# Gated attention block on one core: last group of the batch attention normalised by halves, logits ahead of the turned outputs, the values' bias taken through the head, PE's order at the router written by hand

## The chip, the core and the metric

The kernel runs on one core of a Trainium2 chip. The metric is the time of one execution in microseconds (us) of device time; the runs of the kernel before gave 2961.96, 2963.43 and 2974.54 us, so the median is 2963.43 us. One more execution was taken with the hardware profiler: it took 2965.17 us and its profiled span is 2963.4 us. Engines are called PE (matrix products and transposes), PEld (PE's weight loads), DVE (vector engine), ACT (scalar engine), POOL (GpSimd) and SP (the engine that issues the transfers); SPq is SP's queue.

## What is computed

The reference is one block of a gated cross-attention network over x of shape (8, 512, 256), all in float32, cut here to what the change touches:

```
x  = x + tanh(g_xattn[0]) * relational_cross_attention(layernorm(x), ctx, boxes)   # 16 heads
n  = layernorm(x)
y1 = ln(n + mha(n))                      # 4 heads, attends over the 8 batch rows' axis
gates = softmax(y1 @ wg); idx = argmax   # 8 experts, 512 tokens each
y2 = ln(y1 + gate * expert(y1))          # two matrix products per expert
x  = x + tanh(g_ffn[0]) * y2
q = layernorm(x) @ WQ.T + bQ;  k = ctx @ WK.T + bK;  v = ctx @ WV.T + bV
Z = softmax(q k.T / 16) @ v
x  = x + tanh(g_xattn[1]) * (tile(Z, 8) @ Wl.T + bl)
x  = x + tanh(g_ffn[1]) * spiking_ffn(layernorm(x))
```

Each row of softmax(q k.T / 16) sums to one, so the constant bV passes through it unchanged: Z = softmax(..) @ (ctx @ WV.T) + bV.

## The kernel before, in words

The work goes through four stages, one after the other. First the gated cross-attention with its projections (`project_all`, `gated_cross_attention`), up to about 1980 us of the span. Then `batch_attention`, about 1980 to 2215 us: 32 tiles of 128 tokens in NG = 8 groups of 4. Then `experts`, about 2215 to 2515 us, which begins with the router (`route`). Last comes `tail` (second cross-attention and spiking feed-forward).

**Batch attention.** The work of tile k = 4g + j is put out by `slot(k)`; PE, ACT, DVE and POOL follow the order of the code here (`manual_schedule`), SP's order is a planner's. A slot turns tile k-1's exponentials on PE (`turn`, L763), forms tile k's scores (L737), mixes tile k-2 (`mix`, L806 on PE, the residual sum `res` L807 on DVE), weighs tile k-1 with its values (`weigh`, L774 on PE, then `o` L780 on DVE) and turns these outputs on PE (`turn_out`, L793, copied by ACT L795 to `oT`). On DVE the scores are masked (`sm`, L742) and their maximum taken (`nm`, L748) before ACT exponentiates them (`e`, L752). Beside that, each of the four slots of a group carries a share of other groups: slot j = 0 turns the inputs of group g+1 (L689) and forms the logits of group g-3 (`logits`: 16 PE matmul records into `pl`, L845, and a DVE copy into `lg`, L849), slots 1 and 2 form queries and keys (L699), slot 3 the values (L715, bias added by DVE at L719). The output layer norm of group g-1 runs in slots 1 to 3: `out_stats` (L59 to L62: four pairs of statistics, one small sum, one power on POOL into `ln_rs`) and `out_norm` (two DVE instructions for each tile, L820 and L823, into `y`, and a write to DRAM, L824). `logits_turn` turns two tiles of y on PE (L832) and ACT copies them to `yT` (L836).

After each group, `late.sums(g)` and `late.load(g)` prepare weights of later stages: for g = 2 to 5 a DVE sum over a staged quarter of Wl (`wl`, L1166), for g = 2 also five scalings (L1151); the loads that `late.load` issues go through SP.

**The end of batch attention** (L913 on) finishes tiles 30 and 31, and puts between them the first pieces of other work: the keys and values of the last attention for batch 0, in four pieces by the generator `late.keys(0, ..)`. A piece of `key` is 4 PE matmul records (L1202), an ACT copy with bias into `kT` (L1207) and a write to `ckd`; a piece of `value` is 8 records (L1217), a DVE instruction that adds the bias into `v` (L1222) and a write to `cvd`. The last group's four tiles are normalised together after `out_stats(7)`, and the last `logits` closes the stage.

**Router and experts.** `route` is a chain of some fifty small DVE instructions: softmax and argmax over 8 experts (L986 to L1006, the exponential on ACT, L989), three matmuls that count tokens ahead of each token (`pc`, `pa`, `pb`, L1011 to L1017), a running sum (L1026, L1027), the place of each token (`loc`, `rest`, `col`), and 32 pairs of one-hot tiles (`rows` L1059, `cols` L1064 and L1068, in four parts) whose products on PE (L1072, `pt`) give the token list (`token`, L1076). POOL gathers the rows of each expert's tokens by it (L1261). The keys and values of batches 1 to 4 (`keys(..)`, before the loop over experts) are put out after the router's code, and the planner chooses where PE does them; only SP follows the code. Then 8 experts follow, each with transposes of its tokens (L1278, copied by DVE L1281), L1295 and L1304 on PE; and after them the values, then the keys, of batches 5 to 7 (L1319).

**Tail.** `fetch` gathers the experts' rows for 4 tiles on POOL (L1395); `combine` adds them on DVE (`z`, L1412), takes statistics (L1357 to L1360), adds (L1423, L1426), takes statistics again, and `ln_apply` (`xn`, L1367) gives what PE turns first (`features`, L1379). `head` multiplies by the summed Wl and adds `bl` (L1437).

Of the kernel before, what the change touches and what calls it, by code (L numbers as in the profile page):

```python
# [11 lines left out]
F32 = mybir.dt.float32  # L12
I32 = mybir.dt.int32
AF = mybir.ActivationFunctionType
ALU = mybir.AluOpType
# [4 lines left out]
P = 128  # L20
B, S, D = 8, 512, 256
# [596 lines left out]
def batch_attention(cx, a, y1, lg, x1q, y1d, xf0, late):  # L618
# [6 lines left out]
    with ExitStack() as es:  # L625
# [183 lines left out]

        def out_stats(g):  # L810
            if g >= 0:
                lns["r", g] = cx.stats(wk, ress[g], 4)

        def out_norm(g, j0, j1):
            if g < 0:
                return
            mv, rs = lns["r", g]
            for j in range(j0, j1):
                y = y1[:, 4 * g + j, :]
                nc.vector.scalar_tensor_tensor(  # L820
                    y, ress[g][:, j, :], mv[:, j, 0:1], g1, ALU.subtract, ALU.mult
                )
                nc.vector.scalar_tensor_tensor(y, y, rs[:, j : j + 1], b1, ALU.mult, ALU.add)  # L823
                nc.sync.dma_start(out=yg_[4 * g + j], in_=y)  # L824
# [32 lines left out]
        def slot(k):  # L857
# [6 lines left out]
            if j == 0:  # L864
                in_stats(g + 2)
                first, second = in_turn(g + 1, 0), in_turn(g + 1, 1)
                turn_out(k - 1)
                do(first)
                logits(g - 3)
            elif j == 1:  # L870
# [32 lines left out]
        with tc.manual_schedule(engines=MANUAL | {mybir.EngineType.Pool}):  # L903
# [9 lines left out]
            for g in range(NG):  # L913
                load(g + 3)
                for j in range(4):
                    slot(4 * g + j)
                late.sums(g)
                late.load(g)
            g = NG - 1
            fill = late.keys(0, staged)  # L920
            turn(NK - 1)
# [3 lines left out]
            logits_turn(g - 1, 0)  # L925
            turn_out(NK - 1)
            next(fill)
            logits_turn(g - 1, 2)
            mix(NK - 1)
            out_stats(g)  # L930
            logits(g - 1)
            next(fill)
            next(fill)
            out_norm(g, 0, 2)
            logits_turn(g, 0)
            next(fill)
            out_norm(g, 2, 4)
            logits_turn(g, 2)
            logits(g)


def route(cx, lg, order, pool, gkd):

# [8 lines left out]
    with ExitStack() as es:  # L952
# [151 lines left out]
class Late:  # L1104
# [66 lines left out]
    def load(self, g):  # L1171

        tc, nc, a, pool = self.cx.tc, self.cx.nc, self.a, self.pool
        if g == 1:

            self.matrix("order", "order", 3, P)
            self.matrix("wk", "WKT", 2, D)
            self.matrix("wv", "WVT", 2, D)
            self.matrix("wq", "WQT", 2, D)
            for name, key in (("bk", "bK"), ("bq", "bQ")):  # L1180
                self.w[name] = pool.tile([P, 2], F32, name=name)
                nc.sync.dma_start(out=self.w[name], in_=a[key])
            for name, key in (("bv", "bV"), ("bl", "bl"), ("g2", "g2"), ("b2", "b2ln")):
                self.vector(name, key)
            self.w["wl"] = pool.tile([P, 2, D], F32, name="wl")
# [24 lines left out]
    def value(self, b, m, tile):  # L1210

        nc, w = self.cx.nc, self.w
        pv = tile("p", [P, 2, D])
# [7 lines left out]
        v = tile("v", [P, 2, D])  # L1221
        nc.vector.tensor_tensor(v, pv, w["bv"].unsqueeze(1).to_broadcast([P, 2, D]), ALU.add)  # L1222
        nc.sync.dma_start(out=self.d["cv"][b][:, 2 * m : 2 * m + 2, :], in_=v)

    def keys(self, b, tile):
# [9 lines left out]
def experts(cx, lg, late, moe, gkd, y1d, yd, between):  # L1235

    tc, nc, ident = cx.tc, cx.nc, cx.ident
    with ExitStack() as es:
# [6 lines left out]

        def keys(*bs):
            for b in bs:
                for _ in late.keys(b, staged):
                    pass
# [16 lines left out]
        tokens(0)  # L1266
        keys(*range(1, late.LAST))
        for e in range(NE):
# [396 lines left out]
def flamingo_gated_block(ctx: ExitStack, tc: tile.TileContext, a, out):  # L1665
    nc = tc.nc
# [53 lines left out]
    with ExitStack() as es:  # L1720
# [11 lines left out]
        def load_x1(q):  # L1732
            if q < NQ:
# [59 lines left out]
def _layout(v):  # L1793
# [45 lines left out]
        "WVT": _rows(x["L1_xattn_WV"].T, 2),  # L1839
        "bV": x["L1_xattn_bV"],  # L1840
        "WlT": x["L1_xattn_Wl"].T.reshape(8, 2, P, D).transpose(2, 0, 1, 3),
# [22 lines left out]
```

## Time and profile before

| what | value |
|---|---|
| runs | 2961.96, 2963.43, 2974.54 us (median 2963.43) |
| profiled execution: its time | 2965.17 us |
| profiled execution: its span | 2963.4 us, mean granted clock of PE 0.989 |
| instructions | 39430 |
| PE busy | 2895.3 us (98%) |
| DVE busy | 1836.2 us (62%) |
| ACT busy | 1403.0 us (47%) |
| chain that ended last | PE 77%, DVE 15%, DMA 2% |
| hardware queue of transfers | 375.28 MB, 43.8% of 16 engines' span |

How to read it: a busy share is an average over stages with different limits, so what a change in one stage is worth has to be read from that stage. In a timeline row the first two columns are the start and the length in us, then the engine, the line of the code, the operation, `out<-in`, the sizes and the count; in brackets stands how long the engine had been idle before and what ended the wait. A row with a count above one merges neighbours and spans them all. In a row of stretches the columns are the stretch, its length, busy us and count for PE, PEld, DVE, ACT and POOL, then the clock that PE was granted (1.00 is full), the busy share of the transfer engines and the GB/s that they moved.

### The profile page before, as it was taken

To read this page: it belongs to the slowest core of one execution; us is meant where nothing else is said; L and a number is where in the kernel's file an instruction comes from. 1 tells how busy PE (TensorE), PEld (TensorE's weight loads), DVE (VectorE), ACT (ScalarE), POOL (GpSimd) and SP (SyncE) were. 2 spreads that over 40 slices of the span, in tenths; PEclk is the share of its full clock that TensorE was granted. 3 is DMA by queue.
4 is the path that set the end of the run, shared out by engine and by line. 5 is a ranking of instruction groups with operands and counts; after the bars stand their busy time and mean duration, and the time that the engine had idled before them with its cause. 6 is when DMAs were issued, how large, how long until landed. Compare 5 with 4: busy or idle time off the path is not lost.

```text
span 2963.4 us, 39430 instructions
## 1 busy us (share of the span) xinstructions
PE 2895.3 (98%) x15304; PEld 2118.9 (72%) x15304; DVE 1836.2 (62%) x2875; ACT 1403.0 (47%) x2196; POOL 138.2 (5%) x137
## 2 busy tenths in 40 slices
PE   8999999999999999999999999999989999899998
PEld 3444478888888888888888888867766666456566
DVE  6332177868777777777777777557753012666758
ACT  4332356665656565665656666335531211343434
POOL 2000000000000000000000000000002111212100
PEclk9999999999999999999999999999989999999999
DMA  7785546454545555555555555461113432211000
GB/s 228 222 235 168 184 117 166 132 166 133 163 137 156 143 153 143 155 141 153 146 151 149 144 153 140 127 199 50 43 58 127 156 124 85 100 45 56 30 15 22
DMA packets 269338, 386.18 MB, mean 130 GB/s; under 512 B 55176, under 2 KB 133000, under 8 KB 266336
## 3 DMA queue, kind: packets, MB, share of 16 engines
q1 hardware_dynamic: 266080, 375.28, 43.8%
q0 software_dynamic: 3072, 8.39, 1.0%
q8 instruction: 121, 1.98, 0.3%
q14 instruction: 65, 0.53, 0.1%
HBM read 237.36 MB, written 78.07 MB: 106 GB/s over the span
## 4 chain that ended last, share of the span: by engine, by line
PE 77%; DVE 15%; DMA 2%; issue 2%; ACT 1%; SPq 1%; POOL 0%; DVEq 0%; ACTq 0%; POOLq 0%
PE pg L448 12%; PE po L504 11%; PE pS L468 7%; PE pk L225 6%; PE pT L484 5%; PE ph L1512 4%; PE pw L535 4%; PE ph L1295 4%; PE py L1304 4%; PE py L1527 4%; PE pv L240 3%; DVE nm L472 2%; PE pz L1484 2%; DVE lt L345 2%; PE pq L699 2%
## 5 line engine op out<-in xcount | busy, mean ns | idle before, releaser
L475 ACT ACTIVATE e<-pS,nm 128x512 f32<-128x512 f32 x512 | 323.8, 684 | 577.3 <-DVE nm L472 576.7
L448 PE MATMUL pg<-wst,emb 116*128 116x208 f32 (+1 forms) x2560 | 582.3, 350 | 8.1 <-DVE gate L454 5.9
L448 PEld LDWEIGHTS pg<-wst,emb 116*128 116x128 f32 x2560 | 414.6, 190 | 205.6 <-issue 79.8
L504 PEld LDWEIGHTS po<-v,at 128*128 128x128 f32 x4096 | 493.0, 192 | 0.1
L504 PE MATMUL po<-v,at 128*128 128x65 f32 x4096 | 485.7, 272 | 0.0
L472 DVE TENSOR_REDUCE nm<-pS 128x2 f32<-128x1024 f32 x256 | 312.8, 1222 | 176.0 <-PE pS L468 176.0
L486 DVE SCALAR_TENSOR_TENSOR at<-gate,pT 128x1024 f32<-128x1024 f32 x256 | 311.5, 1217 | 47.6 <-PE pT L484 46.7
L468 PE MATMUL pS<-kT,qT 64*128 64x512 f32 x1024 | 291.6, 641 | 4.2 <-ACT e L475 2.0
L484 PE MATMUL pT<-ident,e 128*128 128x128 f32 x2048 | 267.0, 273 | 0.0
L484 PEld LDWEIGHTS pT<-ident,e 128*128 128x128 f32 x2048 | 240.5, 141 | 14.0 <-DVE o L512 1.5
L454 DVE COPY gate<-pg 128x416 f32<-128x416 f32 (+1 forms) x289 | 165.2, 572 | 50.1 <-PE pg L448 29.8
L454 ACT COPY gate<-pg 128x416 f32<-128x416 f32 x351 | 166.5, 530 | 33.5 <-PE pg L448 31.1
L1308 DVE TENSOR_TENSOR ye<-py,b 128x256 f32<-128x256 f32 x32 | 13.6, 425 | 208.3 <-PE py L1304 208.3
L1299 ACT ACTIVATE hT<-ph,eb 128x512 f32<-128x512 f32 x64 | 44.0, 687 | 178.1 <-PE ph L1295 178.1
L225 PE MATMUL pk<-ctxT,wk__129 128*128 128x512 f32 x256 | 114.5, 603 | 10.0 <-DMA ctxT<-in_ctxT 7.2
L62 POOL TENSOR_TENSOR ln_rs<-ln_ve,mhalf 128x4 f32<-128x4 f32 x24 | 25.1, 1044 | 2059.6 <-DVE ln_ve L61 1999.3
L1512 PE MATMUL ph<-xnT,wf 128*128 128x512 f32 (+2 forms) x320 | 118.7, 513 | 1.8 <-ACT xnT L1382 1.8
L535 PE MATMUL pw<-wo,oT 128*128 128x256 f32 x512 | 117.6, 383 | 0.5 <-ACT oT L527 0.5
L240 PE MATMUL pv<-wv,ctxT 128*128 128x512 f32 x256 | 114.7, 593 | 0.7 <-DVE vs L244 0.6
L1295 PE MATMUL ph<-dT,w 128*128 128x512 f32 x256 | 112.0, 595 | 2.9 <-DVE dT L1281 2.9
L225 PE MATMUL pk<-xnT,wq 128*128 128x512 f32 x256 | 113.0, 594 | 1.1 <-DVE xnT L260 0.6
L468 PEld LDWEIGHTS pS<-kT,qT 64*128 64x128 f32 x1024 | 77.9, 184 | 49.7 <-issue 35.4
(255 smaller groups left out, 3971.8 us busy)
## 6 DMA issues: line engine op xcount, KB each, us to landing
v<-vdr SPq DMA_DIRECT2D x256, 260.0 KB
kT<-kdr SPq DMA_DIRECT2D x256, 256.0 KB
emb<-lt SPq DMA_DIRECT2D x64, 520.0 KB
emb<-nt SPq DMA_DIRECT2D x64, 520.0 KB
vdr<-vs SPq DMA_DIRECT2D x8, 2080.0 KB
kdr<-st SPq DMA_DIRECT2D x64, 256.0 KB
qdr<-st SPq DMA_DIRECT2D x64, 256.0 KB
qT<-qdr SPq DMA_DIRECT2D x32, 512.0 KB
```

Source lines behind the costliest of these rows:

```text
L225: nc.tensor.matmul(pk, w[:, c, m * P : (m + 1) * P], src[:, c, :], start=(c == 0), stop=(c == 1))
L448: nc.tensor.matmul(pg[:, c, 0 : nq * H], embs[i % 2][R, blk // 2, blk % 2, kc * P : (kc + 1) * P], wst[i % 2][R, q0 * H : (q0 + nq) * H], ...
L454: copy(gates[i][:, :, 2 * hf : 2 * hf + 2, q0 : q0 + nq].rearrange("p h k q -> p k h q"), pg[:, :, 0 : nq * H].rearrange("p k (q h) -> p k ...
L468: nc.tensor.matmul(pS[:, t, :], qTs[i][rows, p, :], kT[rows, :], start=True, stop=True)
L472: nc.vector.tensor_reduce(nm, pS, AX.X, ALU.max, negate=True)
L475: nc.scalar.activation(e[:, t, :], pS[:, t, :], AF.Exp, bias=nm[:, t : t + 1])
L484: nc.tensor.transpose(pT[:, t, kc, :], e[:, t, kc * P : (kc + 1) * P], ident)
L486: nc.vector.scalar_tensor_tensor(at, gates[i][:, 2 * p : 2 * p + 2], 1e-6, pT, ALU.max, ALU.mult)
L504: nc.tensor.matmul(po[:, 2 * (p % 2) + t, :], at[:, t, kc, :], v[:, kc, t, :], start=(kc == 0), stop=(kc == NQ - 1),)
L535: nc.tensor.matmul(pw, oT[:, c, :], wo[:, c, :], start=(c == 0), stop=(c == PAIRS - 1))
L1295: nc.tensor.matmul(ph, w1[:, c, f * P : (f + 1) * P], dT[:, c, :], start=(c == 0), stop=(c == 1),)
L1512: nc.tensor.matmul(ph[:, 0:n], wf[:, c, f * P : (f + 1) * P], xnT[:, c, tok], start=(c == 0), stop=(c == 1),)
```

## The change

Four edits, of which the first two are in `batch_attention`.

1. The last group is normalised by halves: `out_stats` and `out_norm` take a first tile and a count. The statistics of tiles 28 and 29 are taken before the end section starts, and these two tiles are normalised after `turn_out(31)`, before the first piece of keys; the statistics of tiles 30 and 31 follow `mix(31)`. The turn of the first half stands before the two pieces of values on PE.
2. In slots j = 0 the logits of group g-3 stand before `turn_out`, not after it. `late.sums(g)` and `late.load(g)`, which stood behind the group's last slot, stand behind slot j = 2 of the next group.
3. The values of the last attention are stored without bias: ACT copies them (it was a DVE sum). `head_bias` forms tanh(g_xattn[1]) * (bV @ Wl) once, on PE in expert 3, and adds it to `bl`; it adds one DVE copy of 128x256, two matmuls of 128x256 and one DVE instruction. `bV` is now loaded as 128x2 instead of a broadcast of 128x256.
4. PE follows the code through the router: `fill(4)` puts the four pieces of batch 1 before the counting matmuls, `fill(5)` puts batch 2 and the first piece of batch 3 before the one-hot products, and the seven pieces that are left come after `route` and before the experts. The pieces of batches 5 to 7 now come batch by batch, keys first.

```
         def slot(k):
...
             if j == 0:
                 in_stats(g + 2)
                 first, second = in_turn(g + 1, 0), in_turn(g + 1, 1)
+                logits(g - 3)
                 turn_out(k - 1)
                 do(first)
-                logits(g - 3)
...
                 for j in range(4):
                     slot(4 * g + j)
-                late.sums(g)
-                late.load(g)
+                    if j == 2 and g:
+                        late.sums(g - 1)
+                        late.load(g - 1)
+
             g = NG - 1
+            out_stats(g, 0, 2)
             fill = late.keys(0, staged)
             turn(NK - 1)
             logits(g - 2)
...
             turn_out(NK - 1)
+            out_norm(g, 0, 2)
             next(fill)
             logits_turn(g - 1, 2)
             mix(NK - 1)
-            out_stats(g)
+            out_stats(g, 2, 2)
             logits(g - 1)
             next(fill)
+            logits_turn(g, 0)
+            out_norm(g, 2, 4)
             next(fill)
-            out_norm(g, 0, 2)
-            logits_turn(g, 0)
             next(fill)
-            out_norm(g, 2, 4)
             logits_turn(g, 2)
             logits(g)
...
         nc.vector.tensor_tensor(hot, ieb, idx.unsqueeze(2).to_broadcast(shape), ALU.is_equal)
+        fill(4)
...
         nc.vector.scalar_tensor_tensor(col, col, 1.0, keep, ALU.add, ALU.mult)
+        fill(5)
         pt = ps.tile([P, NC], F32, name="pt")
...
         v = tile("v", [P, 2, D])
-        nc.vector.tensor_tensor(v, pv, w["bv"].unsqueeze(1).to_broadcast([P, 2, D]), ALU.add)
+        nc.scalar.copy(v, pv)
         nc.sync.dma_start(out=self.d["cv"][b][:, 2 * m : 2 * m + 2, :], in_=v)
+
+    def head_bias(self, pool, ps):
+        nc, w = self.cx.nc, self.w
+        bv = pool.tile([P, 2, P], F32, name="bvr", bufs=1)
+        nc.vector.tensor_copy(bv, w["bv"].unsqueeze(2).to_broadcast([P, 2, P]))
+        pb = ps.tile([P, D], F32, name="py", tag="y")
+        for c in range(2):
+            nc.tensor.matmul(pb, bv[:, c, :], w["wl"][:, c, :], start=(c == 0), stop=(c == 1))
+        nc.vector.scalar_tensor_tensor(
+            w["bl"], pb, self.tg[:, 1:2], w["bl"], ALU.mult, ALU.add
+        )
...
-        token, finish = route(cx, lg, late.w["order"], moe, gkd)
+        pieces = itertools.chain(*(late.keys(b, staged) for b in range(1, late.LAST)))
+
+        def fill(n):
+            for _ in range(n):
+                next(pieces, None)
+
+        token, finish = route(cx, lg, late.w["order"], moe, gkd, fill)
+        fill(4 * B)
+        yield
...
         tokens(0)
-        keys(*range(1, late.LAST))
...
             if e == 3:
-                gslot, gk = finish()
+                result = finish()
+                late.head_bias(wk, ps)
...
-        for fn in (late.value, late.key):
-            for b in range(late.LAST, B):
-                for m in range(2):
-                    fn(b, m, staged)
-    return gslot, gk
+        for b in range(late.LAST, B):
+            for _ in late.keys(b, staged):
+                pass
+    yield result
...
-        with tc.manual_schedule(engines={mybir.EngineType.SP}):
-            gslot, gk = experts(
-                cx, lg, late, moe, gkd, y1d, yd, load_x1
-            )
+        stage = experts(cx, lg, late, moe, gkd, y1d, yd, load_x1)
+        with tc.manual_schedule(engines={mybir.EngineType.SP, mybir.EngineType.PE}):
+            next(stage)
+        with tc.manual_schedule(engines={mybir.EngineType.SP}):
+            gslot, gk = next(stage)
+            stage.close()
```

As built, two orders that the diff does not tell differ too. On ACT the exponential of the router (L989 before) stands behind the first `kT` copy of batch 1; before, it stood ahead of it. On SP the first quarter of the load of x1 (1024 KB), which stood behind all the writes of batches 1 to 4, stands ahead of the writes of batch 1, right behind the last write of batch 0's values.

More of the change, by code (lines that the diff above doesn't have):

```diff
@@ L1 @@
+import itertools
 import math
@@ L807, in mix, with out_stats @@
             nc.vector.tensor_tensor(ress[g][:, j, :], pw, xfs[g][:, j, :], ALU.add)
-        def out_stats(g):
+        def out_stats(g, j0=0, n=4):
             if g >= 0:
-                lns["r", g] = cx.stats(wk, ress[g], 4)
+                lns["r", g, j0] = cx.stats(wk, ress[g][:, j0 : j0 + n], n)
         def out_norm(g, j0, j1):
@@ L816, in out_norm @@
                 return
-            mv, rs = lns["r", g]
+            i0 = j0 if ("r", g, j0) in lns else 0
+            mv, rs = lns["r", g, i0]
             for j in range(j0, j1):
-                y = y1[:, 4 * g + j, :]
+                y, i = y1[:, 4 * g + j, :], j - i0
                 nc.vector.scalar_tensor_tensor(
-                    y, ress[g][:, j, :], mv[:, j, 0:1], g1, ALU.subtract, ALU.mult
+                    y, ress[g][:, j, :], mv[:, i, 0:1], g1, ALU.subtract, ALU.mult
                 )
-                nc.vector.scalar_tensor_tensor(y, y, rs[:, j : j + 1], b1, ALU.mult, ALU.add)
+                nc.vector.scalar_tensor_tensor(y, y, rs[:, i : i + 1], b1, ALU.mult, ALU.add)
                 nc.sync.dma_start(out=yg_[4 * g + j], in_=y)
@@ L929, in batch_attention, with route @@
             mix(NK - 1)
-            out_stats(g)
+            out_stats(g, 2, 2)
             logits(g - 1)
             next(fill)
+            logits_turn(g, 0)
+            out_norm(g, 2, 4)
             next(fill)
-            out_norm(g, 0, 2)
-            logits_turn(g, 0)
             next(fill)
-            out_norm(g, 2, 4)
             logits_turn(g, 2)
             logits(g)
-def route(cx, lg, order, pool, gkd):
+def route(cx, lg, order, pool, gkd, fill):
     tc, nc = cx.tc, cx.nc
@@ L1179, in load @@
             self.matrix("wq", "WQT", 2, D)
-            for name, key in (("bk", "bK"), ("bq", "bQ")):
+            for name, key in (("bk", "bK"), ("bq", "bQ"), ("bv", "bV")):
                 self.w[name] = pool.tile([P, 2], F32, name=name)
                 nc.sync.dma_start(out=self.w[name], in_=a[key])
-            for name, key in (("bv", "bV"), ("bl", "bl"), ("g2", "g2"), ("b2", "b2ln")):
+            for name, key in (("bl", "bl"), ("g2", "g2"), ("b2", "b2ln")):
                 self.vector(name, key)
@@ L1244, in staged @@
             return (kp if name == "p" else kw).tile(shape, F32, name=name, tag=name)
[L1246 to L1249, printed above, removed]
-        token, finish = route(cx, lg, late.w["order"], moe, gkd)
+        pieces = itertools.chain(*(late.keys(b, staged) for b in range(1, late.LAST)))
[5 more added lines that the diff above has]
+        yield
         wk = es.enter_context(tc.tile_pool(name="ewk", bufs=2, reuse_waits="tile"))
@@ L1839, in _layout @@
         "WVT": _rows(x["L1_xattn_WV"].T, 2),
-        "bV": x["L1_xattn_bV"],
+        "bV": x["L1_xattn_bV"].reshape(2, P).T,
         "WlT": x["L1_xattn_Wl"].T.reshape(8, 2, P, D).transpose(2, 0, 1, 3),
```

## The prediction, made before the changed kernel was run

> **What bounds the kernel now.** I read the page first: PE is busy 98% and makes up 77% of the chain that ended last, so the question is where PE idles or runs at a lower clock, and whether the change ends that. A table of stretches shows it in three places only: the starts of the groups in batch attention (from 2050 us), its end with the router (2200 to 2261), and the passage to the tail (2493 to 2521). Two stretches of that table, granted clock third from the end:
>
> ```profile
> 2200.00:2215.00 15.00, 10.40 (x43) 7.45 (x41) 5.48 (x15) 1.86 (x3) 1.01 (x1) 0.82 0.40 123
> ...
> 2234.00:2244.00 10.00, 9.82 (x40) 9.28 (x41) 4.67 (x9) 0.00 (x0) 0.00 (x0) 0.52 0.48 153
> ```
>
> PE is busy 10.40 of 15 us in the first; in the second it is busy throughout, but at half clock. Then I read the timeline of each place. A group's start:
>
> ```profile
> 2050.98 1.91 DVE L1166 TENSOR_REDUCE wl<-y 128x128 f32<-128x1024 f32 x1
> ...
> 2055.81 0.61 PE L793 MATMUL pt<-ident,o 128*128 128x128 f32 x2 [1.60 <-DVE o L780]
> ...
> 2056.21 3.42 PE L845 MATMUL pl<-wg,yT 128*128 128x8 f32 x16
> ...
> 2144.17 1.85 PE L845 MATMUL pl<-wg,yT 128*128 128x8 f32 x16
> ```
>
> DVE's sum of Wl delays `o`; PE waits for it 1.60 us, loses its clock, and the logits take 3.42 us where they take 1.85 at full clock. The end of batch attention and the router:
>
> ```profile
> 2205.86 3.35 PE L1217 MATMUL pq<-wv,ctxT 128*128 128x256 f32 x8
> ...
> 2209.25 0.69 DVE L1222 TENSOR_TENSOR v<-pq,bv 128x512 f32<-128x512 f32 x1 [3.72 <-PE pq L1217]
> 2209.86 0.48 DVE L820 SCALAR_TENSOR_TENSOR y<-res,ln_mv,g 128x256 f32<-128x256 f32 x1
> ...
> 2214.91 0.19 DVE L849 COPY lg<-pl 128x32 f32<-128x32 f32 x1 [3.14 <-PE pl L845]
> ...
> 2234.18 7.04 PE L1072 MATMUL pt<-cols,rows 128*128 128x32 f32 x32 [3.35 <-DVE cols L1068]
> ...
> 2244.14 1.87 PE L1072 MATMUL pt<-cols,rows 128*128 128x32 f32 x16
> ...
> 2261.49 1.04 PE L1278 MATMUL pt<-ident,dt 128*128 128x128 f32 x8
> ```
>
> DVE, in order, holds the last two tiles' `y` behind a `v` whose product PE has not finished; PE then waits for the `y`. In the router PE runs out of keys and values and waits 3.35 us for `cols`, after which 32 records take 7.04 us where 16 take 1.87 at full clock. The passage to the tail:
>
> ```profile
> 2504.10 0.48 DVE L1412 SCALAR_TENSOR_TENSOR z<-yg,gsn,z 128x256 f32<-128x256 f32 x1 [1.19 <-DMA yg<-yd,gslot]
> ...
> 2507.86 0.69 DVE L1222 TENSOR_TENSOR v<-p,bv 128x512 f32<-128x512 f32 x1 [2.08 <-PE p L1217]
> 2508.47 0.42 DVE L1357 BATCH_NORM_STATS2 ln_st<-z 128x6 f32<-128x256 f32 x1
> ...
> 2521.16 1.64 PE L1379 MATMUL pt<-ident,xn 128*128 128x128 f32 x8 [1.94 <-DVE xn L1367]
> ```
>
> Again a `v` stands ahead of the chain that the tail needs.
>
> **The sum, part by part.**
>
> *1. Group starts, idle.* Five slots with logits (tiles 12, 16, 20, 24, 28) wait for `o`: 1.60, 0.74, 0.75, 0.75, 0.56, together 4.40 us. With the logits ahead, 1.85 us of PE work lies in each wait, and the next turn of exponentials still finds `e`: at 2144 `o` ends at 2143.84 and the last `e` before 2144.6, PE would come to it at about 2145.2. The moved sum (1.91 us) falls where DVE idled 1.74 us ahead of `sm` (2161.45), so it delays a slot by 0.2; with the five scalings (3.1 us in all, from 2049.80) by 1.4, of which 1.1 is covered (`o` ended at 2163.81, PE turned it at 2164.93): 0.3 lost, once. Net **-4.1**; bounds -4.4 and 0 (the wait moves to `e`).
>
> *2. Group starts, clock.* From score to score, slots of one kind take 6.78 and 7.13 us at full clock, but 10.12 then 8.16 after tile 12 and 8.78 after tile 16; in the last group four records run at half speed after tile 28 (1.09, 1.23, 2.07, 1.81 for 0.60, 0.71, 1.13, 1.00). Beyond the idle that is 2.5 + 1.0, 1.65, and some 2.5: 7.7 us, at three of the five boundaries. The gaps go, but stretches of short records remain (8 transposes, 16 logits), so I take half, **-3.7**; bounds -7.7 and +3.4 (one more fall, priced as the worst seen).
>
> The row: a gap of 1.60 us was followed by granted clock 0.59, one of 0.75 by 1.00. [...]
>
> *3. End of batch attention.* Key piece 2 ends on PE at 2201.0. Then follow in the new order: 0.6 for four transposes (their `y` is ready by 2196.2: four of 0.48 after `o` at 2194.2), two values 3.45 (16 records at the rate of 2251.31 to 2254.76), 0.6, logits 1.85, copy 0.4: `lg` at 2207.9 for 2215.10. The second half's `y` need `res` at 2198.1, two statistics 1.1, POOL 1.0 and four times 0.48: 2202.3, ahead of their turn at 2205.1. ACT copies two `v` (0.58, as `yT`) just ahead of the last `yT`; the first half of the logits (0.9 us) covers it. **-7.0**; bounds -7.3 and -4 (two half-speed windows as at 2206 and 2213 stay).
>
> *4. Router.* From `lg` (L) to the experts' first transposes 46.2 us before. After: `fill(4)` 3.45 + 3.45 = 6.9; three counting matmuls 1.2 (2222.49 to 2223.7); `tot` at L+8.1, from there to `rest` 6.25 (6.87 less the 0.62 of the `v` at 2225.72) and 3.56 to the first `cols`: L+17.9. PE, with 8.6 us of `fill(5)`, is there at L+16.9: 1.0 idle. 64 one-hot records at 0.117 are 7.5, the seven last pieces 12.1: L+37.5, or -8.7. DVE's parts keep ahead (four parts in some 8 us). The exponential waits behind a `kT` copy (L+2.9 for L+1.2), so `hot` is ready at L+6.9, when PE arrives. A clock fall in the one-hot run costs about 5 (40 records full, 24 at 0.22, 3.4 us of half speed behind). I take 3: **-5.7**; bounds -8.7 and -1. Expert 0's gather (issued 0.94 after `token`, 4 at 1.25, about 2.3 to land: token + 8.2) stays ahead of the 12.1 us of pieces.
>
> Queues: on SP the load of x1 (1024 KB, some 2.8 us at the 380 GB/s of the busiest slices) now stands ahead of batch 1's writes and waits for the last `cvd` write (issue 2206, 2.3 to land); keys have three buffers, so PE needs the first `ckd` only by L+12. The batch-3 context is issued at L+8 and needed at L+15.2.
>
> *5. Head bias.* Four records of 128x256 as L806's four: **+0.9**; DVE's two are off the path. Bounds 0.9 and 1.4 (DVE's copy uncovered).
>
> *6. Passage to the tail.* Statistics start at 2504.6, not 2508.47, and the chain behind them keeps its 12.7 us to PE at 2521.16. PE's pieces at full clock (22 us from 2493.7) end before 2517. ACT takes six `v` beside six `kT` (0.58 and 0.69 in 21 us). **-4.0**; bounds -4.4 and -1 (gathers land later).
>
> Sum: -4.1 - 3.7 - 7.0 - 5.7 + 0.9 - 4.0 = **-23.6**. Against the profiled execution's own 2965.2 (span 2963.4 and 1.8 around it) that is 2941.6; the median of the runs is 1.7 lower, so the median after is 2939.8, and I say **2940**.
>
> **The rivals.** *(a) The clock takes it back.* Part 2 gives 0, the 64 one-hot records fall to half, the end keeps its windows: -4.1 + 0 - 4 - 3 + 0.9 - 2 = -12, about 2951. For it: at 2234 records of 32 columns ran at half for 10 us. Against: at 2244 to 2248 thirty-two of them, with two keys between, ran at full clock.
>
> *(b) Slower: SP holds PE.* x1's first load waits on SP for the release of batch attention's memory; behind it stand `ckd`, `cvd` and the batch-3 context, and PE, now in hand order, cannot pass by to other work as the planner let it. It decides when SP is stuck past L+12 (three key buffers). PE then stands for all beyond that: to lose the 24 us gained and 15 more, SP would have to stay until L+51, about 2251 of the new span; the time would be some 2978. Against: all that it waits for is over near L in the old trace, where a load of this stage (L1389) was issued at 2215.01, just when `lg` was written.
>
> *(c) No effect.* The moved waits come back one for one (PE waits for `e` at group starts, for `hot` and `cols` in the router, for gathers at the tail): 2960. Against: `v` is a real blocker in two places, and it leaves DVE.
>
> **How the numbers follow.** About 0.5% (14.8 us) is what a measurement of this kernel can tell from no change: faster means below 2948.6. Forecast 0.79 (2930 to 2948.6), (a) 0.14 (2948.6 to 2957, a few of them still faster), (c) 0.03, (b) 0.04. Best ends: -4.4 - 7.7 - 7.3 - 8.7 + 0.9 - 4.4 = -31.6, 2932; worst ends 0 + 3.4 - 4 - 1 + 1.4 - 1 = -1.2, 2962. Leaving 2 in 10 outside, the range is 2930 to 2954. Faster 0.80, same 0.16, slower 0.04.
>
> **What would show it.** Right: no wait for `o` at L793 in tiles 12 to 24; `lg`'s last copy at about 2200, some 15 us earlier (parts 1 to 3); no idle over 1.2 us between `lg` and the experts and `token` some 26 us after `lg`; statistics of `z` directly behind the fourth gather. Wrong: half clock over the one-hot products (a); an idle PE at a key piece released by a context transfer or by ACT waiting for `ckd` (b); PE waiting for `e` at L763 after the logits (c).

## The result, and the profile after

The changed kernel ran in 2943.08 us, the median of four runs (2942.12 to 2944.38); beside it on the same chip the kernel before had 2965.03 us. The ratio is **0.9921 [0.9906, 0.9936]**. The forecast was 2940 us with a range of 2930 to 2954, so sign and size were right. Not all of the reasons were.

The profiled execution took 2944.38 us with a span of 2942.6 us, and PE was granted 0.991 of its clock. The new code numbers its lines anew: scores L738, weigh L775, turn of outputs L794, mix L807, y turns L834, logits L847, one-hot L1080, key L1210, value L1226, expert transposes L1302, `ph` L1320, first `xn` transposes L1402.

Four stretches of the profile answer to parts 1 to 6. The first runs from the scores of tile 12 to those of tile 31, the second from there to the last copy into `lg`, the third on to the first product of expert 0 (`ph`), and the fourth, the passage, from the first late piece behind the experts to the first turned `xn`. Every number in the columns of stretches is of one profiled execution, in us:

| kernel | median | ratio to before | tiles 12 to 31 | to `lg` | to `ph` | passage |
|---|---|---|---|---|---|---|
| before | 2965.03 | 1 | 135.50 | 29.21 | 47.93 | 27.24 |
| changed | 2943.08 | 0.9921 [0.9906, 0.9936] | 123.67 | 22.99 | 45.36 | 23.28 |
| c_after (changed, again) | 2944.28 | 0.9917 [0.9893, 0.9942] | 123.66 | 22.98 | 48.63 | 23.48 |
| e1 logits behind | 2944.07 | 0.9921 [0.9898, 0.9944] | 123.23 | 24.65 | 46.96 | 23.31 |
| e2 sums back | 2950.59 | 0.9947 [0.9931, 0.9964] | 129.40 | 24.66 | 46.35 | 23.41 |
| e12 both back | 2951.99 | 0.9949 [0.9929, 0.9968] | 138.55 | 21.63 | 44.72 | 23.41 |
| e3 bias on DVE | 2958.79 | 0.9974 [0.9961, 0.9986] | 123.68 | 22.98 | 49.50 | 37.11 |
| e5 whole group | 2942.73 | 0.9921 [0.9903, 0.9940] | 123.67 | 23.39 | 46.08 | 23.48 |
| e8 bias on DVE, whole group | 2963.70 | 0.9988 [0.9975, 1.0001] | 122.53 | 32.84 | 49.70 | 37.21 |
| e4 planner's PE order | 2940.99 | 0.9917 [0.9898, 0.9936] | 122.52 | 23.24 | 40.32 | 23.30 |
| e6 one more piece | 2940.30 | 0.9911 [0.9892, 0.9930] | 123.73 | 24.64 | 43.99 | 23.54 |
| e7 run broken three times | 2938.13 | 0.9911 [0.9890, 0.9932] | 123.65 | 23.27 | 42.17 | 23.38 |
| e10 run broken late | 2941.78 | 0.9915 [0.9898, 0.9931] | 123.67 | 22.99 | 47.04 | 23.41 |
| e11 combined | 2936.35 | 0.9902 [0.9883, 0.9920] | 123.65 | 22.99 | 39.66 | 23.50 |

The group starts. The first two rows stand where the wait of 1.60 us and the logits of 3.42 us stood before (the timeline of PE, profile of the changed kernel):

```profile
2056.48 1.85 PE L847 MATMUL pl<-wg,yT 128*128 128x8 f32 x16
2058.18 0.41 PE L794 MATMUL pt<-ident,o 128*128 128x128 f32 x2
```

There is no bracket behind L794, so no wait, and the logits take 1.85 us, at full clock (granted 1.00 from 2056 to 2064 us).

The end of batch attention and the router, timeline of PE and DVE:

```profile
2193.73 3.62 PE L1226 MATMUL pq<-wv,ctxT 128*128 128x256 f32 x16
...
2199.61 0.19 DVE L851 COPY lg<-pl 128x32 f32<-128x32 f32 x1 [5.71 <-PE pl L847]
...
2199.85 5.40 PE L1210 MATMUL p<-ctxT,wk 128*128 128x512 f32 x8 [0.28 <-DVE lg L851]
...
2202.55 0.42 DVE L992 TENSOR_REDUCE mx<-lg 128x32 f32<-128x256 f32 x1 [2.75 <-DMA cvd<-v]
...
2219.49 9.73 PE L1080 MATMUL pt<-cols,rows 128*128 128x32 f32 x64 [1.09 <-DVE cols L1076]
...
2229.26 0.19 DVE L1084 CAST token<-pt 128x32 int32<-128x32 f32 x1 [5.76 <-PE pt L1080]
```

The 16 records of values go through in one piece at full clock (granted 1.00 over the 3.62 us), and `lg` is there at 2199.8; the forecast said about 2200. Then three things go wrong. Eight keys take 5.40 us where eight at 2236.9 took 3.60 (granted clock 0.50 from 2200.16 to 2203.57 us). The router's first reduction waits 2.75 us for the landing of the last values. The 64 one-hot records take 9.73 us; at the 1.87 us per 16 of the kernel before they would take 7.5. The two stretches of this part, granted clock third from the end:

```profile
2186.00:2200.00 14.00, 13.72 (x79) 10.96 (x78) 5.87 (x17) 4.85 (x9) 0.70 (x1) 0.98 0.40 106
...
2219.00:2229.00 10.00, 9.51 (x64) 9.51 (x65) 4.47 (x9) 0.12 (x1) 0.00 (x0) 0.75 0.31 100
```

Ahead of `lg` PE is busy 13.72 of 14 us at 0.98 of its clock. In the one-hot run it is busy too, at 0.75.

The passage, timeline of DVE and PE:

```profile
2486.09 0.88 DVE L1435 SCALAR_TENSOR_TENSOR z<-yg,gsn,z 128x256 f32<-128x256 f32 x2 [1.76 <-DMA yg<-yd,gslot]
2486.89 0.42 DVE L1380 BATCH_NORM_STATS2 ln_st<-z 128x6 f32<-128x256 f32 x1
...
2499.58 2.17 PE L1402 MATMUL pt<-ident,xn 128*128 128x128 f32 x8 [2.46 <-DVE xn L1390]
```

The statistics follow the fourth `z` at once. Nothing stands between them.

### The profile page after: what moved, and what is told of

It is laid out like the page before. It is cut to its first block, busy times and chain, and to the rows that moved or that the text cites. A ratio compares the mean times of both kernels' runs of the same rounds, so it can differ in the third digit from the quotient of the medians.

```text
span 2942.6 us, 39447 instructions
## 1 busy us (share of the span) xinstructions
PE 2887.5 (98%) x15308; PEld 2114.9 (72%) x15308; DVE 1826.0 (62%) x2862; ACT 1411.9 (48%) x2212; POOL 138.6 (5%) x138
## 4 chain that ended last, share of the span: by engine, by line
PE 79%; DVE 13%; DMA 2%; issue 2%; ACT 1%; SPq 1%; POOL 0%; ACTq 0%; DVEq 0%; POOLq 0%
PE pg L449 13%; PE po L505 11%; PE pS L469 7%; PE pk L226 6%; PE pT L485 6%; PE ph L1535 4%; PE pw L536 4%; PE ph L1320 4%; PE py L1329 4%; PE py L1550 4%; PE pv L241 3%; DVE nm L473 2%; PE pz L1507 2%; DVE lt L346 2%; PE pq L700 2%
## 5 line engine op out<-in xcount | busy, mean ns | idle before, releaser
L63 POOL TENSOR_TENSOR ln_rs<-ln_ve,mhalf 128x4 f32<-128x4 f32 (+1 forms) x25 | 25.4, 1017 | 2049.4 <-DVE ln_ve L62 1989.2
L1320 PE MATMUL ph<-dT,w 128*128 128x512 f32 x256 | 111.9, 595 | 2.4 <-DVE dT L1305 2.4
```

The source lines that it names most:

```text
L1320: nc.tensor.matmul(ph, w1[:, c, f * P : (f + 1) * P], dT[:, c, :], start=(c == 0), stop=(c == 1),)
```

## The experiments

The theory at the start was the prediction's: each edit gains where the sum put it. The rivals came from the trace: that one edit of a pair does the work of both, and that the clock, not the order, decides the router.

**Group starts: c_after, e1, e2, e12.** c_after is the changed kernel once more, as a measure of chance. e1 puts the logits behind the turned outputs again; e2 puts the sums back behind the group's last slot; e12 does both.

```
e1, e12:      turn_out(k - 1); do(first); logits(g - 3)       # logits(g - 3) stood first
e2, e12:      for j in range(4): slot(4 * g + j)
              late.sums(g); late.load(g)                      # stood behind slot j == 2 of the next group
```

> The changed kernel again, as a yardstick on this chip. Every theory: about 0.992 of the kernel before; from tile 12's scores to tile 31's 123.7 us again if the clock's full speed there is no accident; a few us more, with half clock behind one of the group starts, if it was.

> The changed kernel with the logits behind turn_out again, the sums of Wl left where the change put them. Measure: from tile 12's scores to tile 31's, 135.5 us before and 123.7 after. If DVE's sum was the cause of the late outputs, o comes in time without the logits' cover: 124 to 126, time about 2944. Rival, the cover by the logits is what counts: PE waits some 0.6 us for o at each of the five group starts and the clock falls at some of them: 128 to 133, time about 2949.

> The changed kernel with the sums and loads behind the group's last slot again, the logits left ahead of turn_out. If an idle PE is what costs (gap and clock), the 1.85 us of logits cover what DVE's sum delays, 0.75 to 1.6 us: 124 to 126 us from tile 12's scores to tile 31's, time about 2944. Rival, the stretch of short records drops the clock whatever gap lies in it: half clock at two or three group starts as before, 128 to 133, time about 2949.

> The changed kernel with logits and sums both where they were. If the second edit as a whole made the gain at the group starts: 132 to 136 us from tile 12's scores to tile 31's, with half clock behind two or three group starts, and a time 8 to 12 us over the changed kernel's. Rival, the clock's falls there are chance and only the 4 us of waits belong to the edit: 127 to 130 and 4 us over.

e1 is as fast as the changed kernel, and its starts are as short: from score to score, the slots of tiles 12, 16, 20 and 24 take 5.82 to 5.95 us. e2 and e12 give up 6 to 9 us in the medians, and their slots take 6.21 and 6.78 us where the clock holds. So **the moved sums made the gain**. With the sums away, DVE delivers `o` before PE asks for it, and nothing is left for the logits to cover; the timeline of e1, at the start of tile 16:

```profile
2083.34 0.44 PE L794 MATMUL pt<-ident,o 128*128 128x128 f32 x2
2083.61 1.85 PE L847 MATMUL pl<-wg,yT 128*128 128x8 f32 x16
```

The logits' place is worth 0.57 us a start while the sums are back (6.78 less 6.21), and at tiles 12 to 24 nothing while they are moved. Tile 28 is the exception: no sum stands there in either kernel, e1 waits 0.56 us for `o` as the kernel before did, and its slot takes 5.72 us for 5.15, so there the logits ahead do the work.

e2 missed its expectation of 124 to 126 us, and the trace shows why. With the sums back the logits cannot cover the wait for `o`, because they wait themselves: `pl` uses the same two buffers as `pw` and `po`, and DVE, late with everything, has not yet taken `res` out of `pw`. At tile 12 this costs 0.99 us, and the clock falls behind it (the logits take 2.95 us for 1.85; timeline of PE); at tiles 16, 20 and 24 it is 0.12 to 0.14 us:

```profile
2055.63 2.95 PE L847 MATMUL pl<-wg,yT 128*128 128x8 f32 x16 [0.99 <-DVE res L808]
```

The old place, in e12 at tile 12, shows the wait of the kernel before and the fall of the clock behind it:

```profile
2054.95 0.44 PE L794 MATMUL pt<-ident,o 128*128 128x128 f32 x2 [1.61 <-DVE o L781]
2055.22 3.37 PE L847 MATMUL pl<-wg,yT 128*128 128x8 f32 x16
```

e12 lost the clock near three of its four starts (slots of 9.94, 10.43 and 8.75 us), e2 at one (9.07 us). In all eleven profiles with the sums moved, 44 starts of these four kinds, none did: their slots lie between 5.82 and 5.95 us. e12's 138.55 us lies above the 132 to 136 expected, and above the 135.50 of the kernel before, so the cost of the falls differed between these two executions.

**End of batch attention and passage: e5, e3, e8.** e5 restores the end section of the kernel before (statistics of four tiles, norms between the values). e3 adds the values' bias on DVE again and passes none through the head, with all else as changed. e8 does both.

```
e5, e8:   mix(31); out_stats(g); logits(g - 1); next(fill); next(fill); out_norm(g, 0, 2); logits_turn(g, 0)
          next(fill); out_norm(g, 2, 4); logits_turn(g, 2); logits(g)
e3, e8:   nc.vector.tensor_tensor(v, pv, w["bv"]..., ALU.add)   # for nc.scalar.copy(v, pv); no head_bias
```

> The changed kernel, with the last group of batch attention normalised as a whole again (statistics of four tiles after the last mix, as before). My theory: the stretch from the last tile's scores to the last logits' copy goes from 23.0 us back to about 29 us, with idle time of TensorE before the y turns and logits of 3 to 5 us in sum, and the kernel is 5 to 7 us slower than the changed one (ratio to before about 0.994). Rival: the stretch was shortened by the sums having gone from the place behind the last slot, not by the halves; then it stays within 1 us of 23.0 and the time is that of the changed kernel.

> The changed kernel with the values' bias added on VectorE again (0.69 us per piece) and no bias passed through the head; the last group still by halves, the pieces still keys first, then values. If the halves and the bias each clear VectorE's way in the end of batch attention, either is enough there: the stretch from the last tile's scores to the last logits' copy stays at 23 to 25 us. In the passage to the tail VectorE's order puts the statistics of z behind the additions of the last values, whose matmuls end some 21 us after the last expert: the statistics come some 11 us later than the 10.6 us they had, and the stretch from the late pieces to the first xn transposes goes from 23.3 us to about 34 us. The stretch to the first expert grows by 0 to 3 us (five additions in VectorE's chain). In sum some 13 us slower than the changed kernel, ratio to before 0.996. Rival, the bias was not what held the passage: it stays at 23 us, and the ratio is 0.992 to 0.993.

> Both undone: the values' bias on VectorE and the last group normalised as a whole. Theory: on VectorE the first addition of the values then stands ahead of the last group's norms and the second between them, each waits for TensorE, and the stretch from the last tile's scores to the last logits' copy goes back to 27 to 30 us, as in the kernel before (29.2 us), although undoing the halves alone left it at 23.4 us. The passage as with the bias alone undone, about 34 us. Ratio to before about 0.998. Rival: the moved sums alone shortened the end; it stays at 23 to 25 us, and the time is that of the kernel with the bias alone undone.

e5 refutes the step of the prediction that it was made for. Without the halves the end takes 23.39 us instead of 22.99, and the time is the same. The longest wait for a `y` in its timeline of PE there is this:

```profile
2192.10 0.44 PE L834 MATMUL pt<-ident,y 128*128 128x128 f32 x2 [0.19 <-DVE y L825]
...
2194.54 1.95 PE L847 MATMUL pl<-wg,yT 128*128 128x8 f32 x16
```

e3 shows the other side. With the bias on DVE but the halves kept, the end takes 22.98 us. Only e8, with both undone, loses it (32.84 us, more than the 27 to 30 expected, with PE at half clock over the second values, 3.54 us for 1.89, and the logits, 3.14 us for 1.85). Its timeline, DVE and PE:

```profile
2198.48 0.69 DVE L1230 TENSOR_TENSOR v<-pq,bv 128x512 f32<-128x512 f32 x1 [3.94 <-PE pq L1225]
...
2200.23 0.41 PE L834 MATMUL pt<-ident,y 128*128 128x128 f32 x2 [1.79 <-DVE y L825]
...
2201.33 3.14 PE L847 MATMUL pl<-wg,yT 128*128 128x8 f32 x16
```

DVE stands 3.94 us before the addition, the norms stand behind it, and PE waits 1.79 us for their `y`. **Either edit removes this**: the bias because the addition leaves DVE, the halves because the norms then come ahead of it. Together they gain no more than one.

In the passage e3 lost 13.8 us against the changed kernel (37.11 and 23.28), more than the 11 expected (its additions also stand between the `z`, which wait for gathers, and so hold up the pieces), and the ratio rose to 0.9974 [0.9961, 0.9986]. Timeline of DVE and PE in e3:

```profile
2503.92 0.69 DVE L1231 TENSOR_TENSOR v<-p,bv 128x512 f32<-128x512 f32 x1 [1.03 <-PE p L1226]
2504.53 0.42 DVE L1379 BATCH_NORM_STATS2 ln_st<-z 128x6 f32<-128x256 f32 x1
...
2517.22 2.00 PE L1401 MATMUL pt<-ident,xn 128*128 128x128 f32 x7 [13.34 <-DVE xn L1389]
```

The statistics wait for the last addition, and PE then idles 13.34 us. With keys first, the new order of the late pieces depends on the bias having left DVE. The kernel before, with the additions and with all values first, took 4 us longer in the passage than the changed kernel. What the new order does with the bias away was not tried by itself.

**Router: e4, e6, e7, then e10 and e11.** e4 gives PE's order in the first stage back to the planner. e6 puts one more piece ahead of the one-hot run, which closes the gap of 1.09 us; e7 leaves the gap and breaks the run with a piece after each of its first three parts.

```
e4:   with tc.manual_schedule(engines={mybir.EngineType.SP}): next(stage)     # PE left out
e6:   fill(6)                                                                 # for fill(5), ahead of pt
e7:   if t0 + PART < NT: fill(1)                                              # behind each part of pt
```

> The changed kernel, with TensorE's order in the first stage of the experts left to the planner again (the pieces of keys and values are issued at the same places of the program, only the hand order is gone). My theory: the hand order is what shortened the stretch from the last logits' copy to the first expert's transposes, 46.4 us before and 44.0 us after; without it the stretch goes back to about 46 us, and the whole kernel is 2 to 6 us slower than the changed one (ratio to before 0.993 to 0.994 in place of 0.992). Rival: the half-clock spells take the same from any order, the stretch stays at 43 to 45 us, and the time is that of the changed kernel.

> The changed kernel, with one more piece of keys and values (8 matmuls, about 1.75 us) ahead of the run of 64 one-hot matmuls, so that TensorE has no gap of 1.1 us before it; the run itself stays unbroken. Theory A, the run of short records itself drops the clock: the granted clock falls to half some 4 us into the run all the same, the run takes 9 to 13 us, and only the gap goes, so the stretch from the last logits' copy to the first expert's transposes shrinks from 44.0 us by 1 us or less. Theory B, the gap drops it: the run goes through at full clock in about 7.2 us, the keys behind it take 1.9 us for 4 and not 3.8, and the stretch is 38 to 40 us.

> The changed kernel, with one piece of keys and values (about 1.75 us) behind each of the first three parts of 16 one-hot matmuls; the gap of 1.1 us ahead of the first part stays. Theory A, the unbroken run of short records drops the clock: each part goes through at full clock in about 1.85 us, the pieces between them in 1.75 us, the token lists come some 3 us later than in the changed kernel, and the first expert's transposes come 2 to 4 us earlier, bounded by the gather (stretch 40 to 42 us in place of 44.0). Theory B, the gap drops it: half clock all the same for some 7 to 10 us, stretch 44 us or more.

e6, timeline of PE and then its stretch:

```profile
2220.85 9.53 PE L1080 MATMUL pt<-cols,rows 128*128 128x32 f32 x64
```

```profile
2220.00:2230.00 10.00, 10.00 (x67) 9.52 (x65) 4.36 (x8) 0.71 (x2) 0.00 (x0) 0.77 0.33 122
```

No bracket: the run starts without a gap, PE is busy 10.00 of 10 us, and the granted clock is 0.77 over the stretch all the same; `ph` comes 1.4 us earlier, for the 1.09 us of the gap. e7, timeline of PE:

```profile
2217.08 1.97 PE L1080 MATMUL pt<-cols,rows 128*128 128x32 f32 x16 [1.09 <-DVE cols L1076]
2218.89 1.96 PE L1212 MATMUL p<-ctxT,wk 128*128 128x512 f32 x4
...
2239.02 0.77 PE L1304 MATMUL pt<-ident,dt 128*128 128x128 f32 x5 [1.54 <-DMA dt<-y1d,token]
```

With the gap, but with a piece behind every 16 records, all four parts take 1.87 to 1.97 us, and the granted clock is 1.00 from 2217 to 2235 us. So **here the unbroken run of short records dropped the clock, and the gap of 1.09 us ahead of it did not**: theory A of both. In the nine profiles whose 64 records stood in one run, that run took 9.5 to 13.7 us. What a longer gap does was not tried: in the kernel before, the 32 records behind a gap of 3.35 us took 7.04 us, with 0.50 of the clock granted over all of them. In e7 the token lists are no earlier (31.6 us after `lg`, the pieces lie between), and PE waits at last for the gather.

e4 did not come out as the theory said: 40.32 us to `ph`, not longer than the changed kernel's 45.36. The planner puts its pieces between the one-hot parts too (32 records, 10 of values, 16, 2, 16), and nothing there is slow (3.76, 1.87 and 1.87 us for the one-hot parts); timeline of PE:

```profile
2218.08 3.76 PE L1080 MATMUL pt<-cols,rows 128*128 128x32 f32 x32 [0.23 <-DVE cols L1076]
...
2238.12 0.77 PE L1302 MATMUL pt<-ident,dt 128*128 128x128 f32 x5 [1.96 <-DMA dt<-y1d,token]
```

Its profiled execution (2936.93 us) was the fastest of four, up to 2943.94, so the 40.32 us in the table flatters it; by the medians the hand order and the planner's cannot be told apart. **The hand order of PE gained nothing that was measured.**

e10 was to combine a broken run with a chain that does not wait for the landing of `v`; its router tiles wait tile by tile.

```
e10:  wk = tc.tile_pool(name="rwk", bufs=1, reuse_waits="tile")    # reuse_waits is new
      if t0 + 2 * PART == NT: fill(1)                              # behind a part of pt
```

> The changed kernel with two edits at the router: one piece of keys and values in the middle of the 64 one-hot matmuls, and the router's tiles wait for the earlier holders of their own space alone (in the changed kernel the first reduction of the logits waits 2.75 us for the landing of the last values). Theory: VectorE's chain starts 2.7 us earlier, TensorE has neither the 0.8 to 1.1 us gaps nor the fall to half clock, the run and its piece take 3.8 + 1.9 + 3.7 us, and the first expert's matmuls start 38 to 40 us after the last logits' copy, in place of 45.4 us (changed kernel) and 42.2 us (run broken three times, gather awaited). 5 to 7 us faster than the changed kernel, ratio to before 0.989 to 0.991. Rival: 32 short matmuls in a row are enough to drop the clock, or the gather is then awaited; 42 us or more, and the time of the kernel with the run broken three times.

Both edits missed their aim. The condition puts the piece behind 48 records, not in the middle. And the wait moved on, as the timeline shows:

```profile
2199.93 0.42 DVE L992 TENSOR_REDUCE mx<-lg 128x32 f32<-128x256 f32 x1
...
2204.68 0.42 DVE L997 TENSOR_REDUCE sm<-ex 128x32 f32<-128x256 f32 x1 [3.38 <-ACT ex L995]
...
2219.58 6.33 PE L1080 MATMUL pt<-cols,rows 128*128 128x32 f32 x48 [1.09 <-DVE cols L1076]
```

`mx` follows `lg` at once, but the exponential stands on ACT behind the first eviction of keys (2203.65), and DVE takes up `ex` 4.8 us after `lg`, as in the changed kernel. The wait of 2.75 us for the landing of `v` had therefore cost nothing by itself where the eight keys are slow, as they are in both profiles (5.40 us). The 48 records take 6.33 us in place of 5.6, and the 16 behind the piece 3.46 (granted clock 0.91 from 2220 to 2225 us and 0.50 from there to 2235).

e11 mends both: the tiles of the pieces wait tile by tile too, ACT follows the code as well, and one piece stands behind 24 and one behind 48 records.

```
e11:  rwk and kwk with reuse_waits="tile"; manual_schedule of SP, PE and Activation
      fill(3) for fill(4); fill(6) for fill(5); if t0 + t in (11, 23): fill(1)
```

> The changed kernel with the router's first stage re-cut: its tiles and those of the pieces wait for the earlier holders of their own space alone, ScalarE's order by hand too (so that the exponential of the logits is not behind an eviction of keys), three pieces ahead of the counting matmuls and six behind them, and one piece after 24 and after 48 of the 64 short one-hot records' matmuls counted in records (twelve matmuls each). Theory: the chain of VectorE begins with the logits' copy, the counting matmuls come 5.5 us after it (8.7 us in the changed kernel), the run starts without a gap at about 17.5 us, no record of it runs at half clock, the token lists are there at 29 us (29.5 us in the changed kernel, with a run at half clock and fewer pieces done), and the first expert's matmuls start 39 to 40 us after the logits' copy, bounded by the gather, in place of 45.4 us. 5 to 6 us faster than the changed kernel, 0 to 3 us faster than the run broken three times; ratio to before 0.989 to 0.991. Rival: the clock falls in this order as well (the short records of the counting or 24 in a row are enough), then 43 us or more and no gain over the run broken three times.

Timeline of PE in e11, then the stretch of its one-hot run:

```profile
2215.47 2.76 PE L1080 MATMUL pt<-cols,rows 128*128 128x32 f32 x24
...
2236.70 14.00 PE L1322 MATMUL ph<-dT,w 128*128 128x512 f32 x32 [0.35 <-DVE dT L1307]
```

```profile
2215.00:2226.00 11.00, 11.00 (x79) 9.55 (x77) 3.98 (x7) 1.96 (x3) 0.00 (x0) 1.00 0.39 123
```

Full clock throughout (1.00), `token` at 29.1 us and `ph` at 39.66 us after `lg`, as expected. Two other expectations missed: the counting products come 7.0 us after `lg`, not 5.5, and the one-hot run begins at 18.4 us, not 17.5, since the eight keys behind `lg` took 5.40 us here too. The six runs took 2934.41 to 2940.05 us, median **2936.35**, ratio 0.9902 [0.9883, 0.9920]. That beats the kernel before. Against the changed kernel the medians say 6.7 us and the traces 5.7 us in this stretch, but the intervals of the two ratios overlap, so the order of the two stands on the trace more than on the times.

## Why the prediction was right or wrong, point by point

- **Parts 1 and 2, group starts** (-4.1 and -3.7). Measured together -11.83, close to the best end of -12.1. No wait for `o` is left in tiles 12 to 28, so the idle 4.4 us went; the rest, some 7.4 us, is clock, twice the half that I took. Being so near the best end is in part luck, since the falls of one profile are a draw: the kernel before shows them behind two of the starts at tiles 12 to 24, e12 with the same waits behind three. What failed is the reason of part 1, "with the logits ahead, 1.85 us of PE work lies in each wait": at tiles 12 to 24 e1 has no logits ahead and no wait, and e2, with the logits ahead and the sums back, has the logits waiting for DVE themselves. The moved sum is the cause of 3.84 of the 4.40 us; for the 0.56 us of tile 28 the reason holds. The sum's own cost, put at 0.3 us once, shows as 0.2 us in tile 15 (a slot of 6.91 for 6.71). The falls of e12 lie behind a gap of 1.61 us (logits of 3.37 us for 1.85) and, some 3 us after their ends, behind gaps of 0.74 us (the slots of 10.43 and 8.75 us), and the fall of e6 behind no gap at all (0.77 over its stretch). How long a gap it takes, or whether it takes one, is not shown.
- **Part 3, end of batch attention** (-7.0). Measured -6.2 (the prediction's own rows give -7.2, which it wrote as -7.0); some 1.7 us went to a spell of half clock at 2183 to 2186 (granted 0.50; four mixes in 1.66 us, eight `po` in 1.81, four turns of y in 0.99, for 1.13, 1.00 and 0.60). The mechanism, a `v` on DVE ahead of the `y`, was right. That two edits each remove it, so that the halves are worth nothing beside the bias, I did not see: I timed the new order and never asked which edit bought it.
- **Part 4, router** (-5.7). Measured -2.6 to `ph`, -2.4 to the first transposes (43.98 us after `lg` for 46.39; the prediction read this as 46.2, and a few starts in it are off by some 0.2 us, which changes nothing). This is the term that was mis-sized. Half clock cost 6.5 us against the prediction's best case of 37.5 us, and I had taken 3: 1.8 us at the eight keys behind `lg`, where I had expected no fall, 2.1 in the one-hot run and 2.6 in the pieces behind it. The fall in the run, which I had priced at 5 us, came in every profile with the run unbroken (9.5 to 13.7 us for the 64 records, 7.5 at full clock), and with it `token` stood at 29.5 us after `lg`, not 26. I had not seen either that the router's tiles lie where a `v` was, which makes DVE wait 2.75 us for its landing, but e10 shows that this wait was hidden. Which edit bought the 2.6 us is open: e4, without the hand order, keeps them.
- **Part 5, head bias** (+0.9). Measured: the expert that holds it takes 29.28 us for 29.04. Its four records lie in the wait for `dT`, which every expert has (0.35 us) and which I had not counted as cover.
- **Part 6, passage** (-4.0). Measured -4.0, by the named step.
- **The rest.** Ahead of tile 12 the changed kernel was 2.75 us later, 1.56 of it at a fall of the clock at the start of batch attention (granted 0.50 for 10.2 us there, for 6.8 us in the kernel before), and the tail 0.8 us longer. No edit lies there; over all the profiles the tail takes either 438.8 to 439.8 or 442.2 to 443.2 us. The sum -11.8 - 6.2 - 2.4 + 0.1 - 4.0, with these +3.5, is the -20.8 between the spans. That the total came within 3 us of the forecast is partly luck: the group starts gained 4.0 us more than their two terms and the router 3.3 us less than its own.
- **Rivals.** Of (a) the one-hot fall came, the falls at group starts did not, and 2951 was missed. Its 0 for part 2 was an estimate that no run shows: the clock's share came to some 7.4 us. Of (b) nothing was seen: no piece waits for SP. Of (c) neither: no wait came back one for one.

## What to carry to other kernels

Time an edit by what is late without it while the other edits stay: two that clear the same queue share one gain, and here the halves, the logits' place and the hand order could each be left out at no measured cost, while the moved sums and the bias on ACT could not. An operation in an in-order queue costs what stands behind it: six additions of 0.69 us on DVE cost 13.8 us of the passage, since the tail's statistics stood behind them. And try to break long runs of short matmuls with wide ones, even where PE has no gap: here 64 records took 9.5 to 13.7 us in one run, and 7.4 to 7.6 us in the parts of e4, e7 and e11.

## What the runs showed of the hardware that was not expected

- **The clock fell while PE was busy.** In e6 PE was busy 10.00 of 10 us over the one-hot run, its weight loads 9.52, and the granted clock was 0.77 over these 10 us and 0.53 over the 6 us behind them. Each of these records has weights of 128x128 and 32 columns of output. Runs of 16 to 32 records with wide records between them took what they take at full clock: 1.87 to 1.97 us for 16 in e7, 2.76 us for 24 in e11 (both granted 1.00), 3.76 us for 32 in e4. The run of 48 in e10 took 6.33 us in place of 5.6. The same 64 records in one run took 9.5 to 13.7 us; what sets the record at which the clock falls is not shown.
- **Half clock came in spells of 3.4 to 10.2 us.** Between 2000 and 2262 us the trace of the kernel before grants 0.50 in six spells (3.4 us from 2090.07 and 2206.13, 6.8 us from 2055.94, 2171.99 and 2212.95, 10.2 us from 2233.43), that of the changed kernel in four (3.4 us from 2166.03, 2183.10 and 2200.16, 10.2 us from 2224.06), and 1.00 outside them. In the changed kernel short records stand ahead of all four: 16 logits (128x8) at 2163.03, 2180.96 and 2197.62 us, the one-hot run (128x32) from 2219.49 us. But the other five (2056.48, 2083.46, 2110.23, 2137.01 and 2189.79 us) had full clock behind them. No run was built to find what sets a spell's start or its length.
- **The same short gap has two outcomes.** Behind the last logits PE idles 0.28 us in every profile. The eight keys that follow took 3.70 us in five of the fourteen and 5.40 to 5.98 us in the other nine. In the changed kernel half clock began at 2200.16 us, 0.31 us behind the start of the keys. In the kernel before it had begun ahead of the gap, at 2212.95 us for keys at 2215.16, and in e8 the logits ahead of the gap were slow already (3.14 us for 1.85). What decides between the two is not shown.
- The same kernel's spans differ too: the two profiles of the changed kernel have 2942.6 and 2948.6 us. Of that, 3.3 us lie between `lg` and `ph`, where the one-hot run took 9.73 and 12.82 us, and 2.6 us lie ahead of tile 12, where the cause is open. Stretches had to be compared, not spans.
